# Ten places for fetched rows, and five fetches per four slot tiles in the last expert block

## The chip, the cores and the metric

The kernel runs on one core of one Trainium2 chip. A core has a matrix engine (PE, with weight loads shown apart as PEld), a vector engine (DVE), an activation engine (ACT), a general-purpose engine (POOL) and a queue engine (SP). Each works through its own instruction stream in order and waits for the others by semaphores. Transfers are issued from the SP and the POOL streams and carried by sixteen DMA engines. The metric is the device time of one execution in microseconds (us), less being better. A profile is one further execution, recorded by the hardware; its own time is given beside it.

## The reference, cut to what matters

The reference is a stack of six residual blocks on 8 x 512 tokens of 256 numbers: a first kind of grouped FFN, attention, the first FFN again, then a second kind of grouped FFN (16 experts), attention, and that second FFN again with the same weights. The change is in the code of the second FFN, which the kernel therefore executes twice:

```python
# x: [8, 512, 256]; weights: 16 experts, 4 experts chosen per token
weights, indices = _gate(xt, gate_w)              # four experts and four weights for each token
c = zeros((T, 16)).at[arange(T)[:, None], indices].add(weights)
h1 = einsum('td,edi->tei', xt, w1); h3 = einsum('td,edi->tei', xt, w3)
y = einsum('tei,eid,te->td', silu(h1) * h3, w2, c)  # weighted sum over the four experts
z = silu(xt @ ws1) * (xt @ ws3) @ ws2               # shared expert
return y + z                                        # the block adds half of it to x
```

## The kernel before, in words

All 4096 tokens stay on chip in `x`, as 32 token tiles of 128. The second FFN (class `Grouped`) routes tokens: `routing` computes for each token and each of its four choices a row number `slot` in a table `slots_d` in device memory. `send` scatters the token rows there (four indirect transfers per token tile, issued by POOL). The table has 144 slot tiles of 128 rows, each belonging to one expert. `tile_steps` works through them in a software pipeline: step i transposes slot tile i (`turn`, `L1854`), multiplies tile i-1 by the expert's first two weight matrices (`hide`, `L1872`, with an ACT function and the DVE product `as` at `L1880`), transposes tile i-3 (`back`, `L1884`), multiplies tile i-4 by the third matrix (`give`, `L1892`) and copies that result out of PSUM on DVE (`ys`, `L1902`). PE order gives a limit used below: `hide` of tile j+2 needs a PSUM place that `as` of tile j frees. After each four tiles SP stores `ys` to the result table `ys_d` (`L1904`) and loads the next four input tiles `xs` (`L1838`).

The results come back per token. `gather(t, r)` (`L1610`) is an indirect transfer on POOL that fetches, for token tile t and choice r, 128 result rows into a place `yg`. `add(t, r)` (`L1629`) on DVE multiplies them by the routing weight and adds them to `x`. `collect` makes a list of 136 items in the order of t and r: item n first issues the addition n-8 (of the token tile two before) and then the fetch n = 4t + r. So a fetch stands eight items ahead of its addition in the written order. Three things can hold a fetch back:

- its place: `yg` has `2 * TOPK` = 8 places, so that fetch n waits for addition n-8;
- a written rule, "four transfers at a time": fetch n waits until fetch n-4 has landed;
- the results it reads: `asked` gives the step from which an item may be issued, and the fetch itself waits for the stores of the tiles it needs. Tokens are grouped in three parts. In the last block their tiles are 0-11, 12-19 and 20-31, and `asked` is 71, 118 and 150, so that fetches 0-47 can be issued from step 71, fetches 48-79 from step 118, and fetches 80-127 only after the last of the 148 steps.

The order of every engine is written out by hand (`manual_schedule`), and so the order of these loops is the order of the instructions. The first execution of the second FFN is `ffn1_before`, whose step loop pops two items in every fourth step, thus five items per four steps, while it also loads the weights of the attention that follows (`attn1_weights`). That attention (`attn1`) takes the remaining items beside its own work. The last block is `ffn1_after`. Its step loop pops one item per step. After the loop the shared expert is still to be computed for most tokens (`pump`: pieces of PE work, each followed by its DVE work). With each piece two items are popped, and what is left of the list is popped at the very end. A token tile is stored to the output (`L2116`) when both its shared part and its last addition are done.

`routing` also uses working tiles from a pool with one place per name. Among them are `masked`, `rank16` (the scratch of the top-four search, not read after it), and `score2` (used only for the last of its steps, in the parts after the first).

Of the kernel before, what the change touches and what calls it, by code (L numbers as in the profile page):

```python
# [9 lines left out]
F32 = mybir.dt.float32  # L10
# [10 lines left out]
P = 128  # L21
B, S, D = 8, 512, 256
# [20 lines left out]
E1, INTER, SHARED = 16, 128, 256  # L43
N_GROUPS, TOPK_GROUPS, TOPK = 4, 2, 4
# [17 lines left out]
class Kernel:  # L62
# [157 lines left out]
    def _ffn0(self, ctx, n, beside, known):  # L220
# [350 lines left out]
        for _ in indices(0):  # L571
            pass
        gather(0)
        for _ in indices(1):
            pass
        turn(0, 0)
        for e in range(E0):
            w1, w2 = wts
            if e + 1 < E0:
                wts = weights(e + 1)  # L580
                gather(e + 1)
            if e == E0 // 2:
                beside()
            hidden(e, 0, w1)
            if e == 0:
                turn(0, 1)
            outputs(e, 0, w2)
            if e + 1 < E0:
                turn(e + 1, 0)
            hidden(e, 1, w1)  # L590
            if e + 1 < E0:
                turn(e + 1, 1)
            ahead = indices(e + 2) if e + 2 < E0 else iter(())
            next(ahead, None)
            outputs(e, 1, w2, ahead)
# [765 lines left out]
class Grouped:  # L1361
# [81 lines left out]
    def routing(self, h, lg, pool, row_psum, then):  # L1443
# [3 lines left out]
        HT = self.parts[h]  # L1447
# [18 lines left out]
        masked = pool.tile([P, HT, E1], F32, name="masked")  # L1466
# [59 lines left out]
        jumps = [(limit, jump)]  # L1526
        if h > 0:
# [6 lines left out]
            nc.vector.tensor_scalar(jump, jump, float(SLOTS - 1), float(P), ALU.add, ALU.mult)  # L1534
            jumps.append((limit, jump))
            yield
        beyond = [pool.tile([P, E1, HT], F32, name=x) for x in ("masked", "score2")[: len(jumps)]]
        for b, (limit, jump) in zip(beyond, jumps):
            nc.vector.tensor_tensor(b, at, bc(limit, 2, HT), ALU.is_ge)
            nc.vector.tensor_tensor(b, b, bc(jump, 2, HT), ALU.mult)  # L1540
# [63 lines left out]
    def gather(self, t, r):  # L1604

        nc, tc = self.k.nc, self.k.tc
        self.y[t, r] = self.k.late.tile([P, D], F32, name="yg", bufs=2 * TOPK)
        ready = self.ready[sum(t >= b for b in self.base[1:-1])]
        assert sum(n for _, n in self.stored) >= ready
        inst = nc.gpsimd.indirect_dma_start(  # L1610
            out=self.y[t, r], out_offset=None, in_=self.k.ys_d[:, :],
            in_offset=bass.IndirectOffsetOnAxis(ap=self.slot[:, r, t : t + 1], axis=0),
            bounds_check=SLOTS * P - 1, oob_is_err=True,
        ).ins
        for other in self.got[-4:-3]:
            tc.add_manual_dep(inst, other.name, SYNC, reason="four transfers at a time")

        keep, n = [], 0
        for store, tiles in self.stored:
            if n < ready:  # L1620
                keep.append(store)
            n += tiles
        tc.declare_no_dep(inst, group=f"stored{self.n}", keep=keep, reason="rows of other tiles")
        tc.add_to_no_dep_group(f"got{self.n}", inst)
        self.got.append(inst)
# [294 lines left out]
def advance(steps, n):  # L1920

    for _ in range(n):
        if next(steps, "end") == "end":
            return False
    return True
# [27 lines left out]
def ffn1_before(k, f):  # L1953
# [4 lines left out]
    with ExitStack() as ctx, k.tc.manual_schedule(engines={E.PE, E.DVE, E.Activation, E.Pool, E.SP}):  # L1958
# [23 lines left out]
        for h in range(last):  # L1982
            feed(h)
            routing = f.route(h)
            routed, prepared = False, h + 1 == last
            preparing = f.prepare(h + 1)
            while not (routed and prepared):

                sent = bool(f.waiting or f.of_part[h])
                routed = routed or not advance(routing, 3 if sent or h else 4)  # L1990
                if sent and not prepared:
                    prepared = not advance(preparing, 2)
                pump.run(1)
                f.send_next()
# [3 lines left out]
        load(0)  # L1998
        feed(last)
        routing, more = f.route(last), True  # L2000
        for _ in range(4):
            pump.run(1)
            advance(routing, 3)
            f.send_next()
# [89 lines left out]
def ffn1_after(k, f, out):  # L2094

    E = mybir.EngineType
    nc = k.nc
    rows_out = out.rearrange("(t p) d -> p t d", p=P)
    with ExitStack() as ctx, k.tc.manual_schedule(engines={E.PE, E.DVE, E.Activation, E.Pool, E.SP}):
        f.enter(ctx)  # L2100
        last = len(f.parts) - 1
        a = f.base[last]
        load, step, total = f.tile_steps()
        f.expert_weights()
        load(0)
        f.shared_weights()
        part = f.prepare(last, TT - QT)
        while advance(part, 1):
            pass
        part = f.route(last)  # L2110
        left = {t: 2 for t in range(TT)}

        def done(t):
            left[t] -= 1
            if left[t] == 0:
                nc.sync.dma_start(out=rows_out[:, t, :], in_=k.x[:, t, :])  # L2116

        coming = f.collect(done)
        rest, more = list(range(a // QT)), True


        pump = Pump()
        order = list(range(a // QT, TT // QT)) + list(range(a // QT))

        def hidden(g):
            def turned():
                if g not in f.xnT:
                    f.columns(g)
            hs, os_ = f.shared(g)
            (pe, dve), rest = hs[0], hs[1:]  # L2130
            return [((lambda: (turned(), pe())), dve)] + rest, [
                (pe, (lambda dve=dve, t=g * QT + 2 * i: (dve(), done(t), done(t + 1))))
                for i, (pe, dve) in enumerate(os_)
            ]

        groups = [hidden(g) for g in order]
        pump.feed(groups[0][0])
        for one, two in zip(groups, groups[1:]):
            pump.feed(two[0] + one[1])
        pump.feed(groups[-1][1])  # L2140

        early = 4 * ((TT - a) // QT) - 2
        for i in range(total):
            step(i)
            if f.closed[last] - 3 - early <= i < f.closed[last] - 3:
                pump.run(1)
                pump.flush()
            more = more and advance(part, 3)
            if i % 2:
                f.send_next()  # L2150
            if not more and not f.waiting and rest and i % 4 == 0:
                f.normal(rest.pop(0))
            if i >= f.asked(coming):
                coming.pop(0)()
        while pump.units or pump.pending:
            pump.run(1)

            for _ in range(min(2, len(coming))):
                coming.pop(0)()
        for late in coming:  # L2160
            late()


def tile_kernel(tc, w, out):
    with ExitStack() as ctx:
        k = Kernel(ctx, tc, w)
        with ExitStack() as first:
            pool = first.enter_context(tc.tile_pool(name="a0f", bufs=1))
            got = []
            k.ffn0(0, lambda: got.append(k.attn0_weights(pool)))  # L2170
            k.reload(range(TT // QT))
            k.attn0(got[0])
        k.ffn0(1, lambda: None, TT - QT)

        k.late = ctx.enter_context(tc.tile_pool(name="late", bufs=1))
        k.wide = ctx.enter_context(tc.tile_pool(name="wide", bufs=1))
        one = Grouped(k, 0, (12, 12, 8))
        weights, coming = ffn1_before(k, one)
        two = Grouped(k, 1, (12, 8, 12))
        k.attn1(weights, coming, two)  # L2180
        ffn1_after(k, two, out)
# [73 lines left out]
```

## Time and profile before

| what | value |
|---|---|
| runs of the kernel | median 3924.3 us of three, 3918.76 to 3925.48 |
| the profiled execution | 3897.61 us; its span, first to last instruction, 3895.9 us |
| PE busy in the span | 3567.9 us, 92% |
| DVE, ACT, POOL busy | 2085.6, 1494.5 and 1191.4 us |
| last block, step loop with fetches | about 3692 to 3813 us of the span |
| last block, shared expert | about 3813 to 3877 us |
| last block, what is left | 3877 to 3895.9 us |
| fetches `L1610` | 256 in all, 128 per execution of the block, about 1.02 us of POOL each |

The page counts what an engine executes; a wait is idle time, put down to what ended it. "a <- b" in a group of waits means that a waited for b. In an answer on transfers, "to landing" is the time from the issue of a transfer until its last part has arrived. Times are microseconds from the span's start. DMA share is the mean busy share of the sixteen DMA engines.

### The profile page before, as it was taken

The page shows a single profiled execution, that of the slowest core. Times are in us where ns is not written, and L with a number is a line of the kernel's source. Part 1 is how long each engine was busy: PE and PEld are TensorE (multiplying, and loading weights), DVE is VectorE, ACT ScalarE, POOL GpSimd, SP SyncE. Part 2 cuts the span into 40 slices and gives each one's busy share as a digit, 9 for nine tenths or more (in the row PEclk, how much of TensorE's full clock was granted, in tenths as well). Part 3 has the DMA queues.
Part 4 walks back from the last instruction along what each step waited for, and adds up shares of the span by engine and source line. Part 5 has one row for each costly group of instructions (what it writes and reads, how often), then busy time and mean ns, then how long its engine had stood idle before and what let it go on. Part 6 is the DMA issues. An engine that isn't in the chain of part 4 may idle for free.

```text
span 3895.9 us, 50976 instructions
## 1 busy us (share of the span) xinstructions
PE 3567.9 (92%) x17052; PEld 2100.4 (54%) x17052; DVE 2085.6 (54%) x5532; ACT 1494.5 (38%) x3451; POOL 1191.4 (31%) x1087
## 2 busy tenths in 40 slices
PE   3999988999998499997788999999999999997997
PEld 1666653444444266664467744554444545555785
DVE  7222116666665521212732678777687677664365
ACT  3222222444444322222145444455444444444441
POOL 2433423334331233331552522210100017302366
PEclk7999997999998699998999999999999999998999
DMA  6333326600011233325255811000000001015475
GB/s 204 70 79 65 75 53 221 213 25 15 25 28 49 84 63 74 82 54 128 71 164 175 258 44 33 28 10 1 1 1 1 1 12 65 33 49 156 150 237 153
DMA packets 262992, 316.61 MB, mean 81 GB/s; under 512 B 31696, under 2 KB 232784, under 8 KB 262480
## 3 DMA queue, kind: packets, MB, share of 16 engines
q1 hardware_dynamic: 213584, 212.12, 17.5%
q0 software_dynamic: 49152, 101.24, 10.7%
q8 instruction: 142, 2.33, 0.2%
q14 instruction: 114, 0.93, 0.1%
HBM read 157.81 MB, written 147.06 MB: 78 GB/s over the span
## 4 chain that ended last, share of the span: by engine, by line
PE 65%; issue 12%; DVE 11%; POOL 5%; ACT 4%; DMA 3%; SPq 0%; POOLq 0%; DVEq 0%; ACTq 0%
PE op L548 6%; PE hs L1872 6%; PE hp L535 6%; PE zp L1196 5%; PE sp L1148 5%; PE pq L1123 4%; PE tp L1182 4%; PE pv L1103 3%; PE yps L1892 3%; PE yp L1215 3%; PE st L891 3%; POOL acc_d L555 2%; PE hp L1784 2%; PE pp L743 2%; PE sp L850 2%
## 5 line engine op out<-in xcount | busy, mean ns | idle before, releaser
L1160 ACT ACTIVATE ex<-sp,nmax 128x512 f32<-128x512 f32 x512 | 344.8, 685 | 462.9 <-DVE nmax L1153 462.8
L548 PE MATMUL op<-w,hid 128*128 128x256 f32 x2048 | 456.2, 381 | 0.0
L535 PE MATMUL hp<-exT,w 128*128 128x512 f32 x1024 | 449.5, 597 | 0.0
L548 PEld LDWEIGHTS op<-w,hid 128*128 128x128 f32 x2048 | 385.0, 190 | 57.0 <-issue 7.7
L1610 POOL DMA_INDIRECT yg<-ys_d,slot x256 | 265.8, 1038 | 437.7 <-DVE x L1629 194.0
L555 POOL DMA_INDIRECT acc_d<-ob,idx x128 | 206.9, 1617 | 571.4 <-ACT ob L554 571.4
L553 DVE TENSOR_TENSOR ob<-op,b 128x256 f32<-128x256 f32 x128 | 54.3, 424 | 543.3 <-PE op L548 460.6
L1182 PEld LDWEIGHTS tp<-ident,ex 128*128 128x128 f32 x2048 | 227.3, 141 | 186.7 <-issue 103.8
L535 PEld LDWEIGHTS hp<-exT,w 128*128 128x128 f32 x1024 | 193.8, 191 | 232.6 <-issue 230.7
L1872 PE MATMUL hs<-w_sb,xT 128*128 (+1 forms) x1152 | 306.6, 389 | 9.2 <-DVE as L1880 4.5
L1153 DVE TENSOR_REDUCE nmax<-sp 128x2 f32<-128x1024 f32 x256 | 300.3, 1214 | 14.8 <-PE sp L1148 14.8
L1426 POOL DMA_INDIRECT slots_d<-wide,slot x176 | 177.8, 1010 | 403.0 <-DVE lane L1565 202.1
L539 ACT ACTIVATE hid<-hp,b 128x512 f32<-128x512 f32 x256 | 175.9, 687 | 320.7 <-PE hp L535 320.7
L1182 PE MATMUL tp<-ident,ex 128*128 128x128 f32 x2048 | 279.3, 278 | 14.6 <-DVE eT L209 13.6
L858 DVE CUSTOM_DVE_ANT_0 junk<-sp,mask 128x256 f32<-128x256 f32 (+3 forms) x512 | 249.3, 487 | 76.4 <-PE sp L850 53.2
L1148 PE MATMUL sp<-qk,qk 64*128 64x512 f32 x1024 | 257.9, 623 | 1.9 <-ACT ex L1160 1.9
L1123 PE MATMUL pq<-xnT,wide 128*128 128x512 f32 x512 | 243.5, 600 | 8.1 <-ACT qk L1129 8.1
L1170 DVE TENSOR_SCALAR ex<-ex,rec 128x512 f32<-128x512 f32 x512 | 245.6, 522 | 9.0
L1196 PE MATMUL zp<-eT,v 128*64 128x512 f32 x1024 | 235.3, 600 | 0.0
L906 ACT ACTIVATE ex<-st 128x768 f32<-128x768 f32 (+1 forms) x192 | 168.5, 882 | 161.4 <-DVE st L904 158.9
L554 ACT ACTIVATE ob<-ob,gate 128x256 f32<-128x256 f32 x128 | 65.0, 508 | 412.3 <-DVE ob L553 412.3
L1880 DVE TENSOR_TENSOR as<-sgs,hs 128x128 f32<-128x128 f32 x288 | 82.3, 286 | 260.6 <-ACT sgs L1878 260.4
(343 smaller groups left out, 5769.6 us busy)
## 6 DMA issues: line engine op xcount, KB each, us to landing
xs<-slots_d SPq DMA_DIRECT2D x70, 512.0 KB, 5.5
ys_d<-ys SPq DMA_DIRECT2D x70, 512.0 KB, 3.4
w<-in_W SPq DMA_DIRECT2D x32, 1024.0 KB, 5.9
slots_d<-mask SPq DMA_DIRECT2D x8, 2304.0 KB, 8.6
ys_d<-mask SPq DMA_DIRECT2D x8, 2304.0 KB, 18.0
w_sb<-in_w SPq DMA_DIRECT2D x24, 512.0 KB, 7.7
xn_d<-xn SPq DMA_DIRECT2D x16, 512.0 KB, 3.5
acc_d<-x SPq DMA_DIRECT2D x8, 1024.0 KB, 6.6
```

Of the source, the lines that this page charges most:

```text
L535: nc.tensor.matmul(hp, lhsT=w1[:, c, f * P : f * P + P], rhs=exT[e][:, c, h * CH : h * CH + CH], start=(c == 0), stop=(c == DC - 1),)
L548: nc.tensor.matmul(op, lhsT=hid[h][:, f, i * P : i * P + P], rhs=w2[:, f, :], start=(f == 0), stop=(f == FC - 1),)
L555: inst = nc.gpsimd.indirect_dma_start(out=acc_d[:, :], out_offset=bass.IndirectOffsetOnAxis(ap=idx[:, e, st : st + 1], axis=0), in_=ob, in ...
L858: nc.vector.tensor_tensor_reduce(out=junk[:, :wd], in0=sps[h // 2][:, h % 2, at : at + wd], in1=mask[:, S - wd :], scale=1.0, scalar=NEG, ...
L1123: nc.tensor.matmul(pp, lhsT=(wq, wk)[a][:, k, c * P : c * P + P], rhs=seq[b]["xnT"][:, k, :], start=(k == 0), stop=(k == DC - 1),)
L1148: nc.tensor.matmul(sp[:, j, :], lhsT=q[r, qt * P : qt * P + P], rhs=k[r, :], start=True, stop=True)
L1153: nc.vector.tensor_reduce(m, sp, AX.X, ALU.max, negate=True)
L1160: nc.scalar.activation(ch["ex", 2 * half + i][:, j, :], sps[i][:, j, :], AF.Exp, bias=nmax[i][:, j : j + 1], accum_out=sums[i][:, j : j + 1],)
L1182: nc.tensor.transpose(tp[:, k, :], ch["ex", qt][:, j, k * P : k * P + P], self.ident)
L1196: nc.tensor.matmul(zp[DK1 * j : DK1 * j + DK1, :], lhsT=seq[b]["v", h][:, k, at : at + DK1], rhs=ch["eT"][:, j, k, :], start=(k == 0), sto ...
L1610: inst = nc.gpsimd.indirect_dma_start(out=self.y[t, r], out_offset=None, in_=self.k.ys_d[:, :], in_offset=bass.IndirectOffsetOnAxis(ap=sel ...
L1872: nc.tensor.matmul(hp.rearrange("p a i -> p (a i)"), lhsT=st[j]["xT"][:, c, :], rhs=self.w13[:, st[j]["e"], c, :].rearrange("p e i -> p (e ...
```

## The change

Three edits. `yg` gets ten places in place of eight, so that fetch n waits for addition n-10. To make room, the second table of `routing` takes over the place of `rank16`, and `score2` is gone. The step loop of `ffn1_after` pops two items in each step whose number is a multiple of four, five per four steps in all; the limits in `asked` stay.

```diff
--- before.py
+++ after.py
@@ routing
-        beyond = [pool.tile([P, E1, HT], F32, name=x) for x in ("masked", "score2")[: len(jumps)]]
+        beyond = [pool.tile([P, E1, HT], F32, name=x) for x in ("masked", f"rank{E1}")[: len(jumps)]]
@@ gather
-        self.y[t, r] = self.k.late.tile([P, D], F32, name="yg", bufs=2 * TOPK)
+        self.y[t, r] = self.k.late.tile([P, D], F32, name="yg", bufs=2 * TOPK + 2)
@@ ffn1_after
             if not more and not f.waiting and rest and i % 4 == 0:
                 f.normal(rest.pop(0))
-            if i >= f.asked(coming):
-                coming.pop(0)()
+            for _ in range(1 + (i % 4 == 0)):
+                if i >= f.asked(coming):
+                    coming.pop(0)()
         while pump.units or pump.pending:
             pump.run(1)
```

## The prediction

> **What bounds the kernel now.** The change touches the end of the program, so I read the stretches of the last block first. The columns after the stretch are its length, busy time (and instructions) of PE, PEld, DVE, ACT and POOL, the granted PE clock, the DMA share and GB/s.
>
> ```profile
> 2155.00:2180.00 25.00, 25.00 (x139) 20.99 (x137) 18.33 (x55) 12.21 (x46) 15.08 (x15) 1.00 0.91 303
> 2180.00:2225.00 45.00, 39.76 (x208) 31.77 (x207) 25.63 (x80) 18.41 (x69) 26.84 (x26) 1.00 0.80 252
> 3692.00:3813.00 121.00, 121.00 (x662) 101.25 (x661) 74.66 (x215) 59.08 (x221) 74.25 (x73) 1.00 0.73 227
> 3877.00:3895.90 18.90, 0.00 (x0) 0.00 (x0) 7.05 (x15) 0.00 (x0) 10.53 (x11) 0.57 0.48 143
> ```
>
> In the step loop (third row) PE never idles: 121.00 of 121.00 us. After 3877 PE has nothing left, and only fetches and additions run: 19 us of pure tail. The first two rows are the first block's loop, which already has five items per four steps; I return to them.
>
> Next, the order of POOL in time (start, duration, idle time before it and what ended that).
>
> ```profile
> 3691.90 1.07 POOL L1610 DMA_INDIRECT yg<-ys_d,slot  x1 [50.10 <-DMA ys_d<-ys]
> ...
> 3701.93 1.02 POOL L1610 DMA_INDIRECT yg<-ys_d,slot  x1 [0.30 <-issue]
> 3706.68 1.02 POOL L1610 DMA_INDIRECT yg<-ys_d,slot  x1 [3.73 <-DVE x L1629]
> 3708.30 1.01 POOL L1610 DMA_INDIRECT yg<-ys_d,slot  x1 [0.61 <-DVE x L1629]
> ...
> 3822.74 1.02 POOL L1610 DMA_INDIRECT yg<-ys_d,slot  x1 [0.30 <-issue]
> ...
> 3835.60 1.14 POOL L1610 DMA_INDIRECT yg<-ys_d,slot  x1 [1.09 <-DVE x L1629]
> ...
> 3889.72 1.02 POOL L1610 DMA_INDIRECT yg<-ys_d,slot  x1 [0.30 <-issue]
> ```
>
> The first is fetch 0, 3701.93 is fetch 7, 3706.68 fetch 8, the last fetch 127. Counting along the full list, 3822.74 is fetch 80, the first that needs all results. In the loop a fetch follows the addition that frees its place, one per step of 1.63 us. Without a wait the spacing is 1.02 + 0.30 = 1.32 us. In the tail four fetches wait again for an addition (0.8 us each beyond the 0.30), because additions stand behind DVE work that waits for PE. From fetch 127 to the end of the span 3895.90 - 3889.72 = 6.18 us pass (landing, addition, store).
>
> Last, the waits of the first block's loop, stretch 2155 to 2225 (total us, times, longest), and the landing times there and in the last loop, in that order.
>
> ```profile
> DVE x L1629 <- DMA yg<-ys_d,slot: 14.1, 8, 3.3
> PE hs L1872 <- DVE as L1880: 4.5, 5, 1.7
> ...
> DMA to landing us min/median/max: 2.8/4.5/7.6
> ...
> DMA to landing us min/median/max: 2.9/3.6/6.3
> ```
>
> At five items per four steps the additions there waited 14.1 us for late rows, and PE then waited for DVE. The last block's loop shows no such wait today.
>
> **The change part by part.**
>
> *The routing table.* The instructions, operands' sizes and order stay; only the place differs, and `rank16` is dead when it is reused. The tables are written and read by DVE alone. Cost 0. Some transfers and copies at the entry of the first block get a wait on POOL's older transfers, since tiles moved; the SP load before them in the queue already waits for these. 0 us.
>
> *Ten places in the first block and the attention.* There a held-up fetch starts 0.75 us after the landing of the fetch four before it (for example 2198.65 after 2197.90): the four-at-a-time rule holds it, not its place. In the attention the additions wait for no row (of the 23.0 us that all additions waited for rows, 14.1 lie in the first block and 8.8 in the last). 0 us; bounds -1 and +1, for two fetches earlier at the part's start.
>
> *Items per step, how far it reaches.* 77 items were popped in the loop (steps 71 to 147, one each). Now items 0-47 are popped by step 108, there is a gap until 118, and items 48-79 end at step 143; item 80 may not start before 150. So the loop holds 80 items, only 3 more; 56 remain, 48 of them fetches. This is the whole direct gain in count.
>
> *The tail.* POOL leaves the loop with all of fetches 0-79 issued by about 3810 to 3813 (48 to 79, from 3769, spaced 1.32 to 1.43). Fetch 80 then needs the last store: issued 3814.85, landing in 3.4 us (the median of the three last stores) gives 3818.3, plus 0.75 wake-up = 3819.1. It was 3822.74: 3.6 us earlier. From fetch 80 to 127 took 66.98 us; four waits of 0.8 make 3.1 of it. In the tail an item now stands three places further on, and its place is free two additions earlier, together five of the eight fetches that PE's 11.7 us per shared group pay for. Putting the additions at their present times, fetch n is allowed after about 3815.5 + 1.46 (n - 82): fetch 97, which waited at 3847.30, is allowed at 3837 and issued by POOL's own spacing at about 3842. Only around fetch 118 do the two lines meet, for some 0.5 us. So 66.98 - 3.1 + 0.5 = 64.4 and fetch 127 goes at 3883.5, 6.2 us earlier. The 6.18 us after it stay. PE ends at the same time, since the additions of the tail find their rows landed 4 us or more before. Gain 6.2; bounds 4.4 (three items alone at 11.7/8 us) and 8.
>
> *The loop itself.* 80 items in place of 77 cost DVE three additions of 0.48 us there and three less later; in a step of two additions DVE works 0.29 + 0.42 + 2 x 0.48 = 1.67 us, over four steps 4 x 0.71 + 5 x 0.48 = 5.2 of 6.55 us, so this hides. What does not hide is a late row, as DVE is in order: `as` and `ys` queue behind a waiting addition, and PE's second-next `hide` needs that `as`. The cushion: addition 0 moves from about 3706.0 to 3702.7 (two steps), its row landed at 3694.75, 7.9 us before. Additions then come every 6.55/5 = 1.31 us, while POOL's spacing back to back was (3701.93 - 3691.90)/7 = 1.43 us. The row's own lateness is 2.9 to 6.3 us, the long ones where a store and a load have just been issued. After 47 fetches the cushion is 7.9 - 47 x 0.12 = 2.2 us for a quick row and -1.3 for a slow one. PE absorbs about 1.5 to 2 us of one DVE wait: in the first block the longest, 3.35 us, cost PE 1.68. The fetches 31 to 47 there, after most of the weight traffic, were spaced 24.27/16 = 1.52 us; at that spacing the cushion is gone at fetch 21 to 37. With a row 2 us later than the first as the usual case and 1.5 us absorbed, the loop costs 47 x (spacing - 1.31) - 5.9 - 1.5: nothing at 1.43, 2.5 us at 1.52. I take +2, nearer to the row with the same item rate; bounds 0 and +8 (in the first block 20 steps lost 7.7 us, 40.27 against 20 x 1.63, with 1 MB weight loads that the last block lacks). From step 108 to 118 POOL catches up, so fetches 48-79 start with a full cushion. Traffic rises from 227 GB/s by (4 + 4 + 5)/(4 + 4 + 4), tiles loaded, stored and fetched per four steps, to 246, below the 252 and 303 of the two rows shown.
>
> Two rules of the Trainium skill were weighed. The row: an uncontended fetch lands in 2.8 us, in the loop in up to 6.3. "DMA: Bandwidth & Descriptors", Anatomy of one DMA, gives about 2.0 us plus bytes/436e3, so an estimate of 2.3 us for 128 KB; then four in flight never bind at 1.32 us spacing, the cushion only shrinks 0.01 per fetch and the loop costs 0: 3918. I take the row, which already holds store and load beside it. The second speaks against the change: "SBUF — State Buffer", Who interferes with whom, says that a DVE operation with two operands in SBUF, as these additions are, or in a two-port mode shuts POOL's reads out while it runs. If each fetch lost one addition's 0.48 us, the spacing would be 1.80 us and the loop would lose some 15 us (47 x 0.49, less the cushion of 7.9): 3933. The row: fetches in the loop overlap additions and take 1.02 us; only in the tail do some take up to 1.24, which the 66.98 us already hold. I take the row.
>
> Sum against the span: 3895.9 - 6.2 + 2.0 = 3891.7, or -4.2 us. The runs' median, 3924.3, is 0.7% over the profiled execution (3897.61); the difference carries over as it is: 3920.
>
> **The rivals.**
>
> *No late rows.* If rows land in 4 us or less in the loop, it costs 0 and the tail gives 6 to 8: 3916 to 3918. For it: no addition waits in that loop today. Against it: landings of 5.3 to 6.3 us at a lower rate.
>
> *Slower: late rows hold PE, as in the first block.* An addition waits in DVE's order, PE waits for `as`, in the loop before step 108. The change loses once these PE waits pass 6.2 us, that is, at a fetch spacing above 1.6 us over the first 48 (47 x 0.29 - 5.9 - 1.5 = 6.2). With 8 to 14 us it gives 3926 to 3932. For it: the 14.1 us of waits at the same item rate. Against it: there 1 MB loads came each 13 us.
>
> *It does nothing.* The tail is held by PE's pieces or by something else than fetches, or the last store lands late: 3923 to 3925. Against it: the tail's last 11 fetches are spaced 1.32 to 1.49 us with PE idle.
>
> **How the numbers follow.** Small gain, tail less loop, 3917 to 3924: 0.56; no late rows, some of it with a larger gain: 0.21; slower: 0.15; nothing: 0.08. A measurement of this kernel can tell about 0.2%, 7.8 us, from no change. Faster than 3916.5 takes the whole of the second case and some drift: 0.14. Slower than 3932 takes the far end of the third: 0.11. The rest, 0.75, is within. The likeliest case alone is 3917 to 3924; the range for 8 in 10, with the other cases' near parts, is 3912 to 3930.
>
> **What would show it.** Right: fetch 80 starts some 3.5 us earlier measured from the last store's side (0.75 us after its landing), fetches 80-127 within 65 us, PE's end to the span's end about 13 us in place of 19, ten items instead of 13 after it. The loop: some waits of additions for rows, 1 to 3 us each after fetch 25, PE idle 0 to 4 us between 3692 and 3813. Wrong: PE idle over 6 us there; spacing over 1.5 us; or any change before 3690.

## The result, and the profile after

The changed kernel takes 3941.06 us (median of 10 runs, 3929.15 to 3955.26) where the kernel before took 3920.18 us beside it (10 runs, 3908.71 to 3927.66). The ratio is 1.0051, 95% interval 1.0035 to 1.0068: slower by 0.5%, some 20 us, outside the predicted range. The profiled execution of the changed kernel took 3929.15 us, its span 3927.4 us.

First the stretches of the changed kernel that answer to those shown of before: two of the first block's loop, the last block's step loop with fetches, and what is left after PE's end (length, busy time and instructions of PE, PEld, DVE, ACT, POOL, granted PE clock, DMA share, GB/s).

```profile
2150.00:2175.00 25.00, 23.73 (x125) 18.78 (x123) 15.24 (x45) 10.24 (x39) 14.57 (x15) 1.00 0.80 253
2175.00:2222.00 47.00, 39.30 (x189) 30.00 (x189) 28.36 (x85) 17.35 (x66) 27.79 (x27) 0.96 0.80 250
3698.90:3840.60 141.70, 129.99 (x656) 102.30 (x654) 76.49 (x218) 57.85 (x219) 83.45 (x80) 0.98 0.65 200
3914.00:3927.40 13.40, 0.05 (x1) 0.00 (x0) 6.33 (x13) 0.00 (x0) 6.48 (x6) 0.62 0.52 160
```

The tail after PE's end has shrunk from 19 to 13 us, as predicted. But in the step loop PE, which never idled before, now idles 11.7 us, and its busy time is longer for the same matmuls. DMA moves less per us than before (200 GB/s against 227), so the loop is not held by more traffic.

Next POOL's fetches in order of time: fetches 0, 5, 6 and 7, then 80, then 127.

```profile
3698.56 1.07 POOL L1610 DMA_INDIRECT yg<-ys_d,slot  x1 [48.47 <-DMA ys_d<-ys]
...
3705.24 1.02 POOL L1610 DMA_INDIRECT yg<-ys_d,slot  x1 [0.30 <-issue]
3707.81 1.02 POOL L1610 DMA_INDIRECT yg<-ys_d,slot  x1 [1.54 <-DMA yg<-ys_d,slot]
3709.14 1.02 POOL L1610 DMA_INDIRECT yg<-ys_d,slot  x1 [0.30 <-issue]
...
3847.19 1.02 POOL L1610 DMA_INDIRECT yg<-ys_d,slot  x1 [8.82 <-DMA ys_d<-ys]
...
3921.23 1.02 POOL L1610 DMA_INDIRECT yg<-ys_d,slot  x1 [0.30 <-DVE x L1629]
```

Fetches now follow each other at 1.32 us with single longer gaps; before, they kept one per step of 1.63 us.

Where does PE lose time? The timeline of the changed kernel, one disturbed slot tile and one undisturbed one (start, duration, idle time before it and what ended that).

```profile
3705.42 0.38 PE L1854 MATMUL tpx<-ident,xs 128*128 128x128 f32 x2
3707.26 0.37 ACT L1856 COPY xT<-tpx 128x256 f32<-128x256 f32 x1 [2.66 <-PE tpx L1854]
3707.68 1.13 PE L1872 MATMUL hs<-w_sb,xT 128*128 x4 [1.89 <-ACT xT L1856]
...
3715.76 0.38 PE L1854 MATMUL tpx<-ident,xs 128*128 128x128 f32 x2
3715.98 1.03 PE L1872 MATMUL hs<-w_sb,xT 128*128 x4
3716.23 0.37 ACT L1856 COPY xT<-tpx 128x256 f32<-128x256 f32 x1 [0.38 <-PE tpx L1854]
```

In the undisturbed tile ACT starts its copy 0.09 us after the transposes end (3715.76 + 0.38 = 3716.14, copy at 3716.23). In the disturbed one the transposes end at 3705.80 and ACT starts at 3707.26, 1.46 us after, with nothing else to do; PE then waits 1.89 us for ACT. I call this a late signal and count it for three ACT operations per slot tile, the copy `xT`, the activation `sgs` and the copy `aT`: start, less the later of ACT's previous end and the end of the PE operation it reads, less what is usual; all above 0.2 us are summed. DVE's product `as`, which waits for ACT, starts at most 0.03 us after ACT's end (or after DVE's own work before it) in every tile. It is PE's results that are late.

Does PE finish late, or is its signal late? PE's ends in the record are modelled, but the trace also holds the times at which PE's semaphore was raised. On the page of before all 284 signals of PE in this loop are recorded, and no two stand closer than 0.1 us. In the changed kernel 232 of the 284 are recorded, and 50 of them stand less than 0.1 us behind the one before, down to 0.034; five of them, between 3707.18 and 3707.36, surround the start of the late copy at 3707.26. The instructions that raise this semaphore start at least 0.2 us apart. So results that came one after the other were reported in one go: the report is late. Where on its way it was held is not shown.

It is not the rows. The additions of the changed kernel in a second trace, with what DVE sat idle for before them in the loop:

```profile
L1629 DVE SCALAR_TENSOR_TENSOR x<-yg,coef,x x71: 474/476/517, 3723.6 to 3847.9; 128x256 f32<-128x256 f32 x71
L1629 DVEq EVENT_SEMAPHORE  x53: 21/21/21, 3724.4 to 3847.6; - x53
its engine sat idle before it (us, times) until:
who waited for it (us, times):
```

The third line has no entry beneath it: no addition waited for a row.

Comparing the changed kernel with the page of before misleads by itself. That page is of an execution of 3897.61 us, 27 us below the median of its runs, and it has next to no late signals (0.3 us in this loop, none in the first block's). A run of the kernel before with only the routing table moved takes the same time as before (below) and gives a trace that is like its runs. It stands for "before" from here on. (The page's time, and its number of records, are like those of the one quiet chip described in the last section; which chip it was taken on is not on record.) Stretches run from the first transpose of one slot tile to that of another, in us:

| stretch | page of before | table alone | changed | changed, second trace |
|---|---|---|---|---|
| first block, tile 88 to the last | 97.7 | 106.5 | 111.7 | 108.3 |
| last block, tile 72 to 143 | 116.7 | 120.9 | 138.8 | 139.4 |
| late signals in it (number) | 0.3 (1) | 6.1 (7) | 33.9 (43) | 38.9 (52) |
| tile 143 to the end of the span | 87.0 | 92.5 | 89.8 | 90.0 |
| in it: fetch 80 to 127 | 67.0 | 72.5 | 74.0 | 74.2 |
| in it: PE's end to the end | 19.8 | 19.9 | 13.4 | 13.2 |
| span | 3895.9 | 3915.9 | 3927.4 | 3937.4 |

From the second column to the last the span grows by 21.5 us: 18.5 in the last block's step loop, some 2 in the first block from tile 88 on and 3.6 elsewhere, less 2.5 in the tail. The clock is not the cause: in this loop the granted PE clock was at half for 3.4 us both with the table alone and in the second trace of the changed kernel, and for 6.8 us in the first.

### The profile page after: what moved, and what is told of

It reads as the page before. It is cut to its first block, busy times and chain, and to the rows that moved or that the text cites. A ratio compares the mean times of both kernels' runs of the same rounds, so it can differ in the third digit from the quotient of the medians.

```text
span 3927.4 us, 50967 instructions
## 1 busy us (share of the span) xinstructions
PE 3588.3 (91%) x17052; PEld 2104.1 (54%) x17052; DVE 2090.1 (53%) x5532; ACT 1494.3 (38%) x3451; POOL 1197.1 (30%) x1087
## 4 chain that ended last, share of the span: by engine, by line
PE 66%; issue 12%; DVE 11%; POOL 4%; ACT 4%; DMA 2%; SPq 0%; POOLq 0%; another core or an unknown queue 0%; DVEq 0%; ACTq 0%
PE hs L1872 7%; PE op L548 6%; PE hp L535 6%; PE zp L1196 5%; PE sp L1148 5%; PE pq L1123 4%; PE tp L1182 4%; PE yps L1892 3%; PE pv L1103 3%; PE yp L1215 3%; PE st L891 3%; POOL acc_d L555 2%; PE hp L1784 2%; PE pp L743 2%; PE sp L850 2%
## 5 line engine op out<-in xcount | busy, mean ns | idle before, releaser
L1182 PE MATMUL tp<-ident,ex 128*128 128x128 f32 x2048 | 279.2, 278 | 14.4 <-DVE eT L209 13.4
L858 DVE CUSTOM_DVE_ANT_0 junk<-sp,mask 128x256 f32<-128x256 f32 (+3 forms) x512 | 249.5, 487 | 76.4 <-PE sp L850 53.1
L1872 PEld LDWEIGHTS hs<-w_sb,xT 128*128 128x128 f32 x1152 | 202.8, 196 | 49.5 <-issue 14.9
```

The lines of the kernel that those rows point to most:

```text
L858: nc.vector.tensor_tensor_reduce(out=junk[:, :wd], in0=sps[h // 2][:, h % 2, at : at + wd], in1=mask[:, S - wd :], scale=1.0, scalar=NEG, ...
L1182: nc.tensor.transpose(tp[:, k, :], ch["ex", qt][:, j, k * P : k * P + P], self.ident)
L1872: nc.tensor.matmul(hp.rearrange("p a i -> p (a i)"), lhsT=st[j]["xT"][:, c, :], rhs=self.w13[:, st[j]["e"], c, :].rearrange("p e i -> p (e ...
```

## The experiments

All times are against runs of the kernel before on the same chip. "Loop" is the last block from tile 72 to tile 143, read from one trace per kernel. It was 120.9 us in the run with the table alone. The blocks of code show the lines that differ; what stands around them is left out.

### Which of the three edits

The three runs take the edits apart; ten places don't fit without the moved table, so these two go together. The fourth is the changed kernel again.

```diff
 table alone:
-("masked", "score2")
+("masked", f"rank{E1}")
 places, with the table:
-bufs=2 * TOPK)
+bufs=2 * TOPK + 2)
 rate alone (ffn1_after):
-            if i >= f.asked(coming):
-                coming.pop(0)()
+            for _ in range(1 + (i % 4 == 0)):
+                if i >= f.asked(coming):
+                    coming.pop(0)()
```

> Only the last block's loop is changed: five fetches and additions per four slot tiles, with eight places for rows and the routing table as before. If the denser loop is the cause of the 20 us (theory R), this run is 15 to 25 us slower than before and its TensorE idles or creeps between steps 72 and 150 of the last block, while the first block is as before. If the ten places are the cause (theory P), this run is within 5 us of before, or a few us faster from the three items less in the tail. If the placement of the buffers is the cause (theory A), within 5 us as well.

> Ten places for fetched rows, and with them the routing table in a dead one's place (ten places do not fit without it); the last loop keeps one item per step. Theory P (GpSimd runs further ahead of the additions, more rows are under way, and the other engines' short waits grow): 10 to 20 us slower than before, some 5 to 10 of it in the first block. Theory R (the denser loop): within 5 us of before. Theory A (only addresses): 10 to 20 us slower, and so is the run with the table alone.

> Only the routing table is put in the dead one's place; eight places and one item per step as before. Theories R and P: within 5 us of before. Theory A (the buffers laid out after the table stand at other addresses, and something there costs): 10 to 20 us slower.

> The changed kernel itself once more, for a second trace on the chip that runs the other three: 15 to 25 us slower than before. If the short stalls seen in its first trace (ACT's copy of xnT 5.8 us late in the tail, TensorE idle 10 us in the loop) belong to the kernel, they stand at the same steps again; if they are chance, they stand elsewhere or are absent while the time is still some 20 us longer.

Before took 3921.15 us (29 runs). The table alone: 0.9996 (0.9985 to 1.0008). Places: 1.0005 (0.9995 to 1.0014). The rate alone, with eight places: 1.0032 (1.0021 to 1.0043). All together: 1.0063 (1.0050 to 1.0075). The loop in these runs, in that order:

```profile
3702.50:3823.40 120.90, 119.01 (x641) 99.02 (x640) 71.60 (x206) 57.21 (x214) 71.43 (x71) 0.99 0.71 224
```

```profile
3711.20:3832.60 121.40, 119.30 (x640) 98.90 (x639) 71.77 (x206) 57.15 (x214) 73.05 (x73) 0.99 0.72 225
```

```profile
3701.50:3837.80 136.30, 126.82 (x641) 99.72 (x640) 74.93 (x212) 56.46 (x213) 79.13 (x77) 0.97 0.66 205
```

```profile
3708.10:3847.50 139.40, 126.82 (x641) 99.02 (x640) 74.66 (x213) 56.86 (x213) 81.47 (x79) 0.99 0.66 201
```

The denser loop costs 15.4 us by itself and 18.0 with the ten places. Late signals are 6.1, 7.8, 35.5 and 38.9 us. In the second trace of the changed kernel they stand at other tiles than in the first, but again all through the two dense parts and, but for one within 2 us of fetch 47, not in the gap between fetch 47 and 48, where no fetch runs. So theory R holds for the larger part: the rate, not places or addresses. Together the two parts cost 0.51% and 0.63% in two measurements, by themselves 0.05% and 0.32%; whether they add to more than their sum is within the noise. Ten places are not quite free: over all traces with five items per four tiles in the first block, its stretch from tile 88 is 104.7 to 109.9 us (five traces, mean 107.4) with eight places and 106.9 to 115.6 (nine traces, mean 111.4) with ten. Part of that may come back in the tail (tile 143 to the end 92.5 with the table alone, 89.9 with the places, one trace each).

### Is it the additions, the rate, or the number under way

```diff
 nine per eight tiles:
-            for _ in range(1 + (i % 4 == 0)):
+            for _ in range(1 + (i % 8 == 0)):
 last twelve steps:
+            for _ in range(1 + (i % 4 == 0 and i >= total - 12)):
 three transfers at a time:
-        for other in self.got[-4:-3]:
+        for other in self.got[-3:-2]:
 fewer fetches (gather):
+        if self.n and r == TOPK - 1:
+            self.y[t, r] = self.y[t, r - 1]
+            return
```

> As the changed kernel, but nine fetches and additions per eight slot tiles instead of five per four. Theory S (GpSimd starts a fetch every 1.32 us at best; a step of the loop is 1.63 us, so five per four steps ask for one every 1.30 us and GpSimd is never idle, and only then do the other engines get TensorE's signals late): one every 1.45 us leaves it idle time, so the loop from step 72 to the last is 121 to 125 us instead of 139, the same 80 items are popped, and the whole is 0 to 6 us faster than before. Theory D (each further addition in VectorE's queue costs the loop): the three items cost the same as in the changed kernel, 15 to 20 us slower than before.

> As the changed kernel, but two items in a step only in the last twelve steps of the loop (three times). Theory S: GpSimd is saturated for a few us at most, the loop is 121 to 125 us, the tail's gain stays: 2 to 7 us faster than before. Theory D: the three items cost what they cost in the changed kernel, wherever they stand: 10 to 20 us slower.

> As the changed kernel, but a fetch waits for the third before it instead of the fourth (three transfers at a time instead of four), in both blocks. Theory N (the late signals come from the number of fetches under way): the stalls shrink in loop and tail, 5 to 15 us faster than the changed kernel, unless the fetches get so slow that the tail takes the gain back. Theory S (GpSimd's own work without a gap is what matters): fetches are spaced by the landing of the third one before, so the stalls shrink only where that adds idle time to GpSimd; within 5 us of the changed kernel, or slower through a longer tail.

> As the changed kernel, but in the last block the fourth row of each token is not fetched; its addition uses the third row again. That part of the computation is left out, so only the loop's time is to be read, not the whole. VectorE adds as often as in the changed kernel, GpSimd fetches three quarters as much. Theory S: one fetch every 1.73 us, the stalls go and the loop from step 72 to the last is 118 to 124 us. Theory D (VectorE's additions hold the chain of a slot tile): the loop stays at 135 to 140 us.

Nine per eight: loop 132.5, late signals 32.7 us, 1.0026 (1.0016 to 1.0037), with POOL busy for 78 of the 132.5 us:

```profile
3704.00:3836.50 132.50, 123.89 (x640) 97.74 (x639) 73.17 (x209) 56.26 (x214) 78.17 (x76) 1.00 0.67 210
```

Theory S, that it takes a rate which POOL can't meet, falls: POOL could meet this one, and the loss is still 12 us. The last twelve steps: loop 121.2, late 9.0, 0.9997 (0.9983 to 1.0011). So the same three items cost nothing measurable when they come at the loop's end, and theory D, a price per addition, falls. Fewer fetches with all additions, in a kernel that leaves out every fourth row and of which only the loop is to be read: loop 126.3, late 18.9. Some 13 of the 18.5 us go with a quarter of the fetches, so the fetches, not the additions, make the larger part; the rest, over the 118 to 124 us expected, stays open. Three at a time: late signals drop to 22.0 us, but the loop stays at 136.9 and the whole at 1.0053 (1.0036 to 1.0070): fetches wait longer now, fetch 0 to fetch 48 takes 94.3 us in place of 90.6, and the additions wait 21.8 us for rows, in 14 places, where in the changed kernel none did.

### Is it a POOL without idle time, or fetches out of step

```diff
 pace (gather, on the kernel before; also on nine per eight):
+        tc.add_manual_dep(inst, self.latest.name, SYNC, reason="in step with its slot tile")
 clearing (gather, on the kernel before):
+        if self.n:
+            nc.gpsimd.memset(self.y[t, r], 0.0)
 one per step in the first block (ffn1_before, on the kernel before):
-            for _ in range(1 + (i % 4 == 0)):
+            for _ in range(1):
```

`self.latest` is the product `as` of the newest slot tile.

> The kernel before, with one wait added: each fetch also waits for VectorE's product (as) of the slot tile of its own step. With eight places and one item per step that holds back only fetches that no addition holds back, the first eight above all, which GpSimd otherwise issues 1.32 us apart in one go. Theory U (TensorE's signals come late while GpSimd runs unpaced, fetch on fetch, and not while each fetch starts with its step): the 4 to 6 us of late signals in the first 20 us of the last block's loop go, the loop from step 72 to the last is 116 to 118 us instead of 121, the whole 2 to 6 us faster. Theory W (late signals at the start of the loop come from something else there, such as the stores of the rows): loop 120 to 122 us, the whole within 3 us.

> Nine items per eight slot tiles with ten places, as in the run of nine, and each fetch waits for the product (as) of its own step. Theory U: GpSimd is never more than one fetch ahead or behind, the late signals fall from 33 us to below 8 and the loop from step 72 to the last from 132.5 to 117 to 122 us; the whole 2 to 10 us faster than before. If what counts is that two fetches follow each other within 1.4 us at all (theory T), two in every eighth step still cost about 1 us each: loop 123 to 127 us. If only the rate counts (theory S), 130 to 134 us.

> The kernel before, but in the last block GpSimd first clears the place (128x256, about 0.3 us by other rows of its kind) and then fetches into it: one item per step as before, GpSimd busy for about 1.7 us per step of 1.63 us, fetches 1.6 to 1.75 us apart. If a GpSimd that is never idle is the cause, whatever it does (theory S), the late signals appear in the whole loop as in the changed kernel: 130 us or more from step 72 to the last. If it takes fetches close behind each other (theories T and U), the loop stays at 119 to 124 us, apart from rows that come late through the slower fetches.

> The kernel before, but the first block pops one item per step too (it popped five per four). What is left is popped at the start of the attention, beside its matmuls. Theory S or U: the first block's loop (from step 88 to the last) loses most of its late signals and falls from 106 to 98 to 101 us, the attention's start pays 0 to 4 us for some ten items more, and the whole is 3 to 8 us faster than before. If the first block's idle time comes from rows that land late and not from late signals, it is within 3 us.

The paced loop, and the loop behind the clearing:

```profile
3699.40:3816.00 116.60, 116.60 (x640) 98.05 (x639) 71.49 (x205) 57.18 (x214) 71.64 (x71) 1.00 0.73 231
```

```profile
3704.40:3823.10 118.70, 118.40 (x641) 98.07 (x640) 71.46 (x206) 57.24 (x214) 94.52 (x141) 1.00 0.74 227
```

With the wait, the loop has no idle PE and 0.3 us of late signals; the burst of eight fetches at its start is gone (0.9981, interval 0.9961 to 1.0001). Behind the clearing POOL's busy time rises from 71 to 94.5 us and it waits for another engine only once (2.1 us), but its fetches start 1.62 us apart at the nearest, and late signals are again 0.3 us. So it is not POOL's load. That kernel's whole is 1.0015 (1.0000 to 1.0031), because fetches 80 to 127 take 78.2 us at this spacing. Nine per eight with the wait: loop 129.3, late 27.8, 1.0018 (1.0005 to 1.0031), a miss for theory U as I wrote it. The trace says why: after many of the pairs POOL catches up with fetches 1.32 us apart, so that four still start within 4.2 us in ten places of the loop, against 14 without the wait.

One item per step in the first block shortens its stretch from tile 88 from 106.5 to 98.0 us, and the whole to 0.9984 (0.9969 to 0.9998):

```profile
2147.40:2245.40 98.00, 93.19 (x496) 75.88 (x496) 59.16 (x177) 43.95 (x166) 54.35 (x55) 1.00 0.79 254
```

So the same loss had been in the kernel before, on these chips, in its other dense loop.

### How close is too close

```diff
 pairs (on the kernel before, with the wait of pace):
-            if i >= f.asked(coming):
-                coming.pop(0)()
+            for _ in range(2 * (i % 2 == 0)):
+                if i >= f.asked(coming):
+                    coming.pop(0)()
 nine with a gap (gather, on nine per eight):
+        if self.n:
+            nc.gpsimd.memset(self.y[t, r][:, :64], 0.0)
 both: pace, and one per step in the first block, on the kernel before
 all: both, with table, places and the last twelve steps of above
 other point of the step (on places with the table):
+        tc.add_manual_dep(inst, self.copied.name, SYNC, reason="in step with its slot tile")
```

`self.copied` is ACT's copy `xT` of the newest slot tile.

> The kernel before with the added wait on the step's product (as), but its one item per step comes as two items in every second step: the same fetches, additions and bytes per us, GpSimd idle for more than half a us after each pair, and some 38 fetches 1.32 us after the one before. Theory T (each close pair costs, some 0.45 us of the loop and 0.8 us of late signals): the loop from step 72 to the last is 128 to 138 us, and 10 to 20 us slower than before. Theory S' (only a stretch in which GpSimd never catches up costs): 117 to 122 us, within 4 us of before.

> Nine items per eight slot tiles with ten places, and in the last block GpSimd clears 64 of the 256 columns of the place before each fetch (0.1 to 0.15 us), so that fetches are never nearer than about 1.44 us; asked for is one every 1.45 us. If 0.12 us more between fetches is enough, the late signals go: loop from step 72 to the last 117 to 123 us instead of 132.5, the whole 4 to 12 us faster than the run of nine. If the signals are late whenever GpSimd is behind, whatever the gap: 129 to 134 us.

> The kernel before with one item per step in the first block too, and with the added wait on the step's product (as): no two fetches close together in either loop. Theory T: the first block's loop from step 88 on is 97 to 99 us (106.5 before), the last block's from step 72 on 116 to 118 (121 before), the attention's start pays up to 2 us; the whole is 8 to 14 us faster than before. If the gains were chance of single traces, it is within 4 us.

> As the run before it, with the ten places, the table in the dead one's place and two items in three of the last twelve steps of the loop, so that the tail has three items less. Theory T: some ten close pairs at the end of the loop cost 3 to 5 us there, the time from TensorE's end to the end falls from 20 to 13 us but TensorE's own tail grows by 3 to 7 us as in the other runs with ten places; the whole is 8 to 16 us faster than before, and within 4 us of the run without these parts.

> Ten places, one item per step, and each fetch also waits for ACT's copy of the transposed slot tile of its own step (xT), so that it starts some 0.9 us after the step's first transpose. If fetches at that point of the step make TensorE's signals late (theory B, bad points), the late signals fill the last block's loop: 124 to 140 us from step 72 to the last, and 5 to 20 us slower than before. If only fetches without a rhythm do (theory U), the loop is 116 to 119 us and the whole 0 to 6 us faster than before.

Pairs: loop 121.9, late 13.0, 0.9989 (0.9976 to 1.0002). Theory T falls: a close pair by itself does not cost. The late signals all stand in the first 60% of the loop (up to 3772 us), where rows of fetches catch up; after them the fetches mostly alternate between 1.45 and 1.8 to 1.95 us, and none is late. (Pairs as close as 1.32 us, with room around them, did not come about.) Nine with a gap of 1.46: loop 125.5 instead of 132.5, late 24.3, 1.0010 (0.9997 to 1.0023): better, not cured.

```profile
3694.80:3820.40 125.60, 122.53 (x642) 97.86 (x640) 73.31 (x210) 56.36 (x214) 90.98 (x149) 1.00 0.71 220
```

The other point of the step was missed, since the fetches came to stand 1.1 us after the tile's first transpose in place of 0.9; loop 118.8, late 10.4, 1.0001 (0.9988 to 1.0013). It can't decide on bad points of the step. But nine with a gap holds a row of seven fetches at 0.7 to 0.8 us after the first transpose, 1.56 to 1.75 us apart and without a late signal, which speaks against them. And the trace of the other point of the step shows how the loss keeps itself going. POOL's fetches in it:

```profile
3736.37 1.02 POOL L1610 DMA_INDIRECT yg<-ys_d,slot  x1 [1.30 <-ACT sgs L1879]
3737.69 1.02 POOL L1610 DMA_INDIRECT yg<-ys_d,slot  x1 [0.30 <-DVE x L1630]
3739.02 1.02 POOL L1610 DMA_INDIRECT yg<-ys_d,slot  x1 [0.31 <-DVE x L1630]
3741.42 1.02 POOL L1610 DMA_INDIRECT yg<-ys_d,slot  x1 [1.39 <-ACT sgs L1879]
3742.74 1.02 POOL L1610 DMA_INDIRECT yg<-ys_d,slot  x1 [0.30 <-issue]
3744.16 1.02 POOL L1610 DMA_INDIRECT yg<-ys_d,slot  x1 [0.40 <-DVE x L1630]
3746.50 1.02 POOL L1610 DMA_INDIRECT yg<-ys_d,slot  x1 [1.32 <-ACT sgs L1879]
```

Three fetches at 1.32 to 1.42 us, a late signal and a gap of 2.3 to 2.4 us, then three close ones to catch up, and so on for some 55 us, at one item per step.

That suggests a measure over several fetches. For every fetch of the last block's loop in the 18 traces from chips with late signals, I take the time from the third fetch before it to itself, and ask whether a signal due in the 1.3 us after it is late; fetches with a late signal in the us before are left out.

| four fetches started within | late signal follows | the same in the first block, from tile 88 on |
|---|---|---|
| 3.9 to 4.2 us | 40 of 44 | 72 of 92 |
| 4.2 to 4.4 | 22 of 27 | 26 of 37 |
| 4.4 to 4.6 | 19 of 39 | 13 of 28 |
| 4.6 to 4.8 | 12 of 65 | 11 of 30 |
| 4.8 to 4.95 (one per tile) | 6 of 408 | 5 of 39 |
| over 4.95 | 59 of 479 | 75 of 506 |

Five per four tiles puts four fetches into 3.9 to 4.0 us, nine per eight into 4.4, one per tile into 4.9. This is theory V: a backlog of fetches. It fits the runs best of the forms tried, and pace, clearing, last twelve and the first block's rate changed the spacing by hand and moved the late signals with it. It is not the whole: over 4.95 us late signals are more frequent again, nearly all of them in loops that are dense elsewhere (in the paced, the cleared and the first combined kernel 3 of 73). What builds up in the chip was not shown.

The two combined kernels: both, 3901.85 us against 3918.64 (33 runs), 0.9957 (0.9944 to 0.9970), faster than either kernel of this case.

```profile
2151.80:2246.30 94.50, 91.92 (x497) 75.86 (x496) 59.12 (x177) 43.96 (x165) 55.17 (x54) 1.00 0.83 264
3693.50:3810.30 116.80, 116.80 (x641) 98.16 (x640) 71.57 (x205) 57.24 (x213) 71.30 (x70) 1.00 0.75 233
```

The two stretches give 12.0 and 4.1 us of the 16.8. With places and the last twelve steps added it is 3904.40, 0.9960 (0.9945 to 0.9975): loop 118.9, tile 143 to the end 89.4 in place of 92.9, no gain that can be told apart.

### The changed kernel with its fetches held apart

```diff
 on the changed kernel (gather):
+        if self.n:
+            nc.gpsimd.memset(self.y[t, r], 0.0)
```

> The changed kernel, five items per four slot tiles and all, but in the last block GpSimd clears the place (0.33 us) before each fetch, so that fetches start 1.62 us apart at the nearest (four in 4.86 us). If the late signals come from how closely the fetches follow each other (theory V, backlog), they fall from 39 us to below 6, although items are asked for as densely as before; rows come later then (48 fetches take 78 us where the additions ask for them in 63), so some additions wait, and the loop from step 72 to the last is 117 to 126 us instead of 139. The whole: within 5 us of before. If the late signals come with the dense items as such, the loop stays above 132 us.

It took 3910.15 us against 3898.70 for the kernel before beside it, 1.0036 (1.0019 to 1.0052). This run fell on a chip on which the kernel before takes 22 us less than on the others. Its trace has no late signal in this loop and 0.3 us of them in the first block's, where from tile 88 on four fetches start within 4.2 us in 25 places. (The page of before has 21 such places there and no late signal.) So the run can't tell what holding the fetches apart does to late signals in the changed kernel. It shows the other half of the expectation, rows that come late when they are fetched at 1.62 and asked for at 1.31 us:

```profile
3682.20:3805.00 122.80, 118.41 (x641) 98.11 (x640) 74.13 (x212) 57.29 (x215) 98.63 (x145) 1.00 0.71 223
```

```profile
its engine sat idle before it (us, times) until:
  DMA yg<-ys_d,slot: 13.6, 8
```

The additions waited 13.6 us in eight places, and the loop took 122.8 us where the page of before has 116.7. From tile 143 to the end it took 97.8 us in place of 87.0, since fetches 80 to 127 take 78.7 us at this spacing in place of 67.0. So this kernel was slower by more than the 5 us allowed for.

## Why the prediction was wrong

*The routing table, 0 us.* Right: 0.9996.

*Ten places in the first block, 0 within 1 us.* Too small a bound. I excluded an effect because the four-at-a-time rule binds and not the place. On the chips with late signals the two further places let fetches run closer, about 4 us by the means above.

*Items per step.* Right: 80 items in the loop.

*The tail, -6.2 us.* Half right. Fetch 80 starts 9.6 us after tile 143 in place of 13.8, 4.2 us earlier where 3.6 was predicted, and the 6.18 us after the last fetch stayed 6.2. PE's end to the end became 13 us, as written. But fetch 80 to 127 was to shorten to 64.4 us; it took 74.0, and 72.5 with the table alone. PE's end did not stay: its time from tile 143 grew from 72.7 to 76.4. In one place PE idles 6.42 us before a group of the shared expert, with ACT's copy 5.8 us behind the transposes it reads. From tile 143 to the end 2.7 us were gained; with the rate alone it was 7.4 (85.1 us against 92.5). These are single traces, whose tails hold late signals of their own.

*The loop, +2 us, 0 to 8.* This is the step that failed: 18 us, 15.4 of it from the rate alone. It searched the price where the first block's waits pointed, in rows that land late, and the sum had no term for PE's reports reaching ACT late. No addition of this loop waited for a row; over the whole program the additions waited 3.9 us for rows in the changed kernel's first trace, 23.0 on the page of before. The slower rival had the sign and the place, but the same wrong mechanism, and its point of decision, a spacing above 1.6 us, was not reached: fetches 0 to 47 took 73.7 us, 1.57 each. The held-apart run on the quiet chip, at a spacing of 1.62, and the run with three transfers at a time show such row waits to be real.

*"The difference carries over as it is."* This step let the other fail. The page lay 27 us below the median of its own runs. I took that for a constant. It was a sign that the runs hold a cost which the page doesn't show, and the change added to just that cost: the first block's dense loop is 97.7 us on the page and 106.5 in a trace like its runs, a third of the difference.

*The rules that were weighed.* The estimate of 2.3 us for a fetch, from the Trainium skill's "DMA: Bandwidth & Descriptors", Anatomy of one DMA, foresaw no row waits and a free loop. There were no row waits in the changed kernel, but the loop was not free, and the shortest landing in the rows shown is 2.8 us. POOL shut out by additions ("SBUF — State Buffer", Who interferes with whom), with a spacing of 1.80 us, did not come: fetches beside additions still start 1.32 us apart. That its sum, 3933, lay nearest is chance.

My own signs for "wrong" did appear, all three: PE idle over 6 us in the loop (11.7), a spacing over 1.5 us (1.57), and changes before 3690.

## What to carry to other kernels

Compare a page's time with its runs before reading costs from it: where it lies well below them, the costs that grow with a change may be the ones it lacks, and a page of the common kind should be read first. Indirect fetches issued one per step of the main loop cost next to nothing here, while more of them, in bursts of four within 4.4 us, stretched TensorE's loop by up to 15% on the chips whose traces lost records. On the one chip that lost none, and on the page of before, 46 bursts of four within 4.2 us in the first block went without a late signal. It may pay to tie such fetches to the step with a wait, and to let the rest run where TensorE doesn't need the time. The wait together with one item per step in the first block made the kernel 0.43% faster; the wait alone, 0.19%, can't be told from none, and no further place or earlier fetch gained anything.

## What the runs showed of the hardware

- PE's results reached ACT late in the step loops, up to 2.6 us in the last block's, on all chips named on record but one: after 62 of 71 groups of four indirect transfers started within 4.4 us, and after 6 of 408 at 4.8 to 4.95 us. DMA share and GB/s were lower, not higher, in these loops.
- One chip of those used showed none of it and ran the kernel before in 3898.70 us where the others took 3918 to 3925. Its trace and the page of before hold 21,699 and 21,698 records of landed transfer parts, the others some 16,000 to 16,900 of the same transfers. So lost records and late signals go together here. The Trainium skill ("NOTIFIC — the notification-queue block", 7.1 Overflow) says that a full ring of such records, by its setting, either loses some or stalls what writes them; that the recording itself makes the signals late is therefore possible, and no run here shows it. Every run that is timed here also gives its span and clock, so the times may hold for recorded executions only. What the changed kernel would do on the quiet chip stays open as well; it was not run there.
- After an idle time PE was slower for a while. In the changed kernel's tail the 16 matmuls after 6.42 us of idle time took 10.20 us, the same 16 otherwise 7.13. The granted PE clock was 0.50 between 3873.50 and 3877.00 us, and 1.00 between 3900.00 and 3907.00:

```profile
3873.55 10.20 PE L1784 MATMUL hp<-xnT,ws_sb 128*128 128x512 f32 x16 [6.42 <-issue]
...
3900.01 7.13 PE L1784 MATMUL hp<-xnT,ws_sb 128*128 128x512 f32 x16 [0.24 <-issue]
```

- POOL starts an indirect transfer of 128 rows every 1.32 us at best: 1.02 us of its own time and 0.30 us between two.
